# Normed lines of the attention stage: a buffer of their own, written and stored in quarters

## The chip, the cores and the metric

One core of a Trainium2 chip. The metric is device time in microseconds (us), the median of three executions; one further execution was profiled, and all durations below are from that one.

## What is computed

The input x is 8 images of 128 x 128 pixels with 64 channels, float32. Two layers follow each other. The first is criss-cross attention: each pixel attends to its column and to its row.

```python
energy_H = jnp.einsum('bhwd,bkwd->bhwk', Q, K)      # diagonal set to -inf
energy_W = jnp.einsum('bhwd,bhvd->bhwv', Q, K)
att = softmax(concatenate([energy_H, energy_W], axis=-1), axis=-1)
x = gamma[0] * (out_H + out_W) + x                  # sums of V by both parts of att
```

The second layer begins with a normalization over the channels, `(x - mu) * rsqrt(var + EPS)`, and goes on with a two-dimensional Fourier transform, a dense layer with GELU, the inverse transform and a convolutional MLP. The change lies between the two: in the lines of normed x that the first layer leaves for the second.

## The kernel before

Two stages run one after the other, `attention` and `mixer`. Between them lie two arrays in HBM: x2, the result of the attention, and xn, the same with the inverse root of the variance multiplied in, in the order [row, half of the columns, channel, 64 columns].

**Tasks.** The attention goes through 64 tasks: 8 images, for each image four blocks of 32 columns ("H", numbered H0 to H3 here) and then four blocks of 32 rows ("W", W0 to W3). A block of the input is one buffer xb of 128 x 2048. W blocks come from a pool of six such buffers (`a_xw`), four used per image, in rotation. Each task spreads over several turns of a loop (lines 599 to 657), which works on several tasks at once. In turn n:

- PE turns the xb of task n + 1 round (`turn`, L348), computes queries, keys and values for it and its energies (L433); DVE takes their maxima (L438), ACT the exponential (L444).
- PE multiplies attention and values for task n, and ACT copies the sums from PSUM to SBUF (`attend`, L403 and L409): into yh for an H block, into yw for a W block. The pool has two yw buffers, each for a pair of W blocks (W0 with W1, W2 with W3). So the first pair of an image takes the buffer of the first pair of the image before. PSUM has four buffers, and the energies need one that L409 has emptied.
- POOL computes the difference of the maxima for task n (`maximum`, L484), ACT the weights for task n - 1 (`weigh`, L514 to L516), POOL their totals (L522 to L524), and POOL merges task n - 2 (`combine`): for each eighth of the block it scales yh and yw (L541), adds each to xb (L544), and stores xb to x2 (L545).
- ACT and DVE square and sum the xb of task n - 4 (L559 to L562); the squares go to yw, whose sums are used up by then.
- POOL takes the inverse root for task n - 5 (`inverse_root`, L89 to L105) and, where that task is the second of a pair, multiplies both blocks of the pair by it (L574, eight instructions of 128 x 512, four for each block) and stores the pair (L578, 2048 KB). The products are written into the same yw buffer, ordered by channel.

At the begin of each image's W blocks PE also turns yh round in place (`across`, L584 and L585); L497 is the copy just ahead of that, and occurs once per image.

**Order.** On PE, ACT, DVE and POOL the order of instructions is the program's. The fetches of xb (L265 for H, L268 for W) are on SP's queue, in an order that the scheduler chose: four of H, then four of W, in turn. A W fetch waits until the last reader of its buffer is through, so the fetches of W2 and W3 of an image wait for the products of W0 and W1 of the image before, and those of W0 and W1 of the next image for the products of W2 and W3. For the last three tasks, DVE and SP take the place of POOL (`merger`, `store`), so 14 pairs are multiplied and stored by POOL and two by DVE and SP.

Of the kernel before, what the change touches and what calls it, by code (L numbers as in the profile page):

```python
# [22 lines left out]
F32 = mybir.dt.float32  # L23
# [3 lines left out]
ALU = mybir.AluOpType  # L27
# [4 lines left out]
P = 128  # L32
C = 64
D8 = 8
HID = 128
R = 32
# [49 lines left out]
def inverse_root(engine, fused, s, q, t):  # L86

    e = engine
    e.tensor_tensor(t, s, s, ALU.mult)  # L89
    e.tensor_scalar(q, q, 1.0 / C, EPS, ALU.mult, ALU.add)  # L90
    if fused:
        e.scalar_tensor_tensor(out=q, in0=t, scalar=-1.0 / (C * C), in1=q, op0=ALU.mult, op1=ALU.add)
    else:
        e.tensor_scalar(t, t, -1.0 / (C * C), None, ALU.mult)
        e.tensor_tensor(q, q, t, ALU.add)
    e.tensor_scalar(s.bitcast(I32), q.bitcast(I32), -0.5, float(0x5F3759DF), ALU.mult, ALU.add)
    e.tensor_scalar(q, q, -0.5, None, ALU.mult)
    for _ in range(3):
        e.tensor_tensor(t, s, s, ALU.mult)
        e.tensor_tensor(t, t, q, ALU.mult)  # L100
        if fused:
            e.scalar_tensor_tensor(out=s, in0=t, scalar=1.5, in1=s, op0=ALU.add, op1=ALU.mult)
        else:
            e.tensor_scalar(t, t, 1.5, None, ALU.add)
            e.tensor_tensor(s, s, t, ALU.mult)  # L105
# [136 lines left out]
def attention(tc, nc, x, w_q, b_q, w_k, b_k, w_v, b_v, gamma, x2, xn, prm, marks, packed):  # L242
    NB = x.shape[0]
    with ExitStack() as ctx:
# [4 lines left out]

        late = ctx.enter_context(tc.tile_pool(name="a_late", bufs=2))  # L250
        xw = ctx.enter_context(tc.tile_pool(name="a_xw", bufs=6))

        ps = ctx.enter_context(tc.tile_pool(name="a_ps", bufs=4, space=PSUM))

# [71 lines left out]
        for n in range(3):  # L326
            m = const.tile([P, 4, 32], F32, tag="m%d" % n, name="m")
# [119 lines left out]
        state = {}  # L447
# [52 lines left out]
        def merger(n):  # L500

            return nc.vector if n >= len(tasks) - 3 else nc.gpsimd
# [5 lines left out]
        def is_w(n):  # L508
            return 0 <= n < len(tasks) and tasks[n][1] == "W"
# [37 lines left out]
        def norm_step(n, part):  # L547


            m = n - 4  # L550
            if is_w(m):
                s = state[m]
                h = slice(16 * (part // 2), 16 * (part // 2) + 16)
                sq = s.y[:, h, 0:C]
                if part % 2 == 0:
                    if m >= N - 3:
                        nc.vector.tensor_tensor(sq, s.xb[:, h, :], s.xb[:, h, :], ALU.mult)
                    else:
                        nc.scalar.activation(sq, s.xb[:, h, :], AF.Square)  # L559
                    nc.vector.tensor_reduce(s.t[:, 0, h], s.xb[:, h, :], AX.X, ALU.add)  # L560
                else:
                    nc.vector.tensor_reduce(s.t[:, 1, h], sq, AX.X, ALU.add)  # L562
            m = n - 5
            if is_w(m):
                b, way, blk = tasks[m]
                s = state[m]
                r, q, t = (s.t[:, i, :] for i in range(3))
                if part == 3:
                    inverse_root(merger(m), m >= N - 3, r, q, t)
                if part == 3 and blk % 2 == 1:  # L570
                    z = s.yw.rearrange("p r c -> p (r c)")[:, 0 : 2 * R * C].rearrange("p (c r) -> p c r", c=C)
                    for o, lo in ((state[m - 1], 0), (s, R)):
                        for h in range(0, R, 8):
                            merger(m).tensor_tensor(  # L574
                                z[:, :, lo + h : lo + h + 8].rearrange("p c r -> p r c"), o.xb[:, h : h + 8, :],
                                o.t[:, 0, h : h + 8].unsqueeze(2).to_broadcast([P, 8, C]), ALU.mult,
                            )
                    (nc.sync if m >= N - 3 else nc.gpsimd).dma_start(out=xn[b][:, blk // 2, :, :], in_=z)  # L578

        def across(o, c0):  # L580

# [14 lines left out]
        N = len(tasks)  # L596
        E = mybir.EngineType
        with tc.manual_schedule(engines={E.PE, E.Activation, E.DVE, E.Pool}):
            for n in range(-1, N + 6):
# [31 lines left out]
                if new is not None or old is not None:  # L631
                    for k in range(2):
                        energies(0, k, new, old, masked)
                norm_step(n, 0)
                if is_w(n - 1):
                    weigh(n - 1)
                if new is not None:
                    new.values(1)
                norm_step(n, 1)
                if old is not None:  # L640
                    target(n)
# [3 lines left out]
                if new is not None or old is not None:  # L645
                    for k in range(2):
                        energies(1, k, new, old, masked)
                norm_step(n, 2)
                if is_w(n - 1):
                    total(n - 1)  # L650
# [679 lines left out]
@with_exitstack  # L1330
def attention_mixer_kernel(ctx: ExitStack, tc: tile.TileContext, x, w_q, b_q, w_k, b_k, w_v, b_v, gamma, *rest):
    nc = tc.nc
    *prm, tbl, marks, out = rest
    NB = x.shape[0]
    dram = ctx.enter_context(tc.tile_pool(name="dram", bufs=1, space=DRAM))
    x2 = [dram.tile([P, P, C], F32, tag="x2_%d" % b, name="x2_%d" % b) for b in range(NB)]
    xn = [dram.tile([P, 2, C, 64], F32, tag="xn_%d" % b, name="xn_%d" % b) for b in range(NB)]
    packed = dram.tile([P, PACKED + ADDED], F32, tag="packed", name="packed")

    spread = dram.tile([32, C], F32, tag="spread", name="spread")  # L1340
    nc.sync.dma_start(out=spread, in_=prm[-1].unsqueeze(0).to_broadcast([32, C]))
    attention(tc, nc, x, w_q, b_q, w_k, b_k, w_v, b_v, gamma, x2, xn, prm, marks, packed)
    mixer(tc, nc, x2, xn, tbl, packed, spread, out)
# [32 lines left out]
```

## Time and profile before

| what | us |
|---|---|
| median of three runs | 3188.97 (3185.77 to 3190.28) |
| the profiled execution | 3192.64 |
| its span | 3190.9 |
| PE busy | 2919.0 (91%) |
| DVE busy | 2470.8 (77%) |
| ACT busy | 2097.3 (66%) |
| POOL busy | 1640.7 (51%) |
| L574, POOL, 112 multiplies of 128 x 512, mean | 1.1 each |
| L578, POOL, 14 stores of 2048 KB, issue to landing | 9.5 each |

The shares are means over two stages with different limits: attention ends near 1350 us, and the mixer, with DVE busy nearly throughout, takes the rest. A line of a wait reads "who waited <- for whom: us in total, times, the longest". In a timeline a line gives start, duration, engine, line of the program, operation, tiles (written <- read), and in brackets the idle time before it with what ended it. The chain of waits is followed back from the last instruction, at each step to what released it. PEld is PE's loading of weights, POOLq and SPq are the queues of POOL and SP.

### The profile page before, as it was taken

Reading aid. Unit: us, or ns where it says so; the run is one execution under the profiler, and the core shown is the slowest. Engines: PE = TensorE matmul, PEld = TensorE weight load, DVE = VectorE, ACT = ScalarE, POOL = GpSimd, SP = SyncE. Lnnn points to the kernel's source line nnn. Section 1 sums busy time; section 2 is a strip of 40 time slices with the busy share of each in tenths; the row PEclk is TensorE's granted clock in tenths of the full one; section 3 lists DMA queues with packets and bytes.
Section 4 is the critical chain, followed back from the end, with each engine's and each line's share of the span. In section 5 each row is a group of like instructions: output and inputs, shape, how many; then the busy total and the mean of one; then the engine's idle time right before and its main releaser. Section 6 shows DMA issues by size and latency. Waiting matters only on the chain.

```text
span 3190.9 us, 110456 instructions
## 1 busy us (share of the span) xinstructions
PE 2919.0 (91%) x50476; PEld 2138.6 (67%) x50476; DVE 2470.8 (77%) x2281; ACT 2097.3 (66%) x2776; POOL 1640.7 (51%) x1974
## 2 busy tenths in 40 slices
PE   7998989898989896999999999999999999999978
PEld 5777777777767775676566575575675675665644
DVE  4575747474747577819999999999999999999996
ACT  3665656565656664538868867767867777777754
POOL 1095959595959585424625516515525525435421
PEclk8999999999999998999999999999999999999989
DMA  6024242424243323242674664654745745745545
GB/s 175 23 96 121 96 134 95 121 96 124 102 138 106 112 95 115 89 159 54 137 166 87 157 146 83 172 117 93 179 106 111 171 99 113 179 94 101 119 90 100
DMA packets 227070, 372.72 MB, mean 117 GB/s; under 512 B 143401, under 2 KB 176812, under 8 KB 208044
## 3 DMA queue, kind: packets, MB, share of 16 engines
q0 software_dynamic: 37072, 188.39, 26.0%
q1 hardware_dynamic: 188764, 177.19, 19.7%
q8 instruction: 396, 6.49, 0.8%
q14 instruction: 70, 0.57, 0.1%
q10 hardware_dynamic: 768, 0.07, 0.0%
HBM read 170.96 MB, written 102.26 MB: 86 GB/s over the span
## 4 chain that ended last, share of the span: by engine, by line
PE 40%; DVE 28%; POOL 18%; issue 6%; DMA 5%; ACT 3%; SPq 0%; POOLq 0%; ACTq 0%; DVEq 0%
DVE acc L1144 19%; POOL xb L544 7%; PE fcps L838 5%; PE dps L906 3%; PE yp L403 3%; PE yps L893 3%; PE e L433 3%; POOL yh L541 3%; POOL yw L541 3%; PE yps L895 3%; DMA acc<-pr 3%; PE op L1206 2%; PE tpy L584 2%; PE vps L381 2%; DMA xn<-yw 2%
## 5 line engine op out<-in xcount | busy, mean ns | idle before, releaser
L1144 DVE SCALAR_TENSOR_TENSOR acc<-h,pk,acc 128x1024 f32<-128x1024 f32 x840 | 1262.6, 1509 | 51.2 <-ACT acc L1130 29.6
L854 POOL TENSOR_TENSOR gs<-gl 128x512 f32<-128x512 f32 (+2 forms) x272 | 447.8, 1665 | 296.7 <-ACT gl L848 295.7
L838 PE MATMUL fcps<-f,pk 128*128 128x512 f32 (+2 forms) x1088 | 506.7, 596 | 0.2 <-ACT f L828 0.2
L438 DVE TENSOR_REDUCE m<-e 128x8 f32<-128x1024 f32 x256 | 302.8, 1214 | 209.4 <-PE e L433 204.8
L444 ACT ACTIVATE att<-e 128x1024 f32<-128x1024 f32 x256 | 259.8, 1024 | 163.6 <-PE e L433 159.7
L848 ACT ACTIVATE gl<-fcps,pk 128x1024 f32<-128x1024 f32 (+2 forms) x272 | 290.0, 1073 | 95.2 <-PE fcps L838 75.6
L433 PE MATMUL e<-qt,kt 32*128 32x128 f32 x4096 | 301.4, 291 | 40.5 <-ACT yw L409 35.2
L1039 POOL TENSOR_TENSOR xc<-x,st 128x512 f32<-128x512 f32 x128 | 181.9, 1436 | 297.0 <-PE tpn L1073 120.3
L1138 POOL DMA_DIRECT2D acc<-pr x120 | 105.6, 880 | 434.6 <-DVE acc L1144 253.0
L403 PEld LDWEIGHTS yp<-v,att 128*64 128x64 f32 x8192 | 264.6, 140 | 88.7 <-issue 41.0
L838 PEld LDWEIGHTS fcps<-f,pk 128*128 128x128 f32 x1088 | 190.8, 192 | 195.0 <-issue 145.2
L433 PE MATMUL e<-kt,qt 32*128 32x128 f32 x4096 | 305.6, 291 | 7.8 <-issue 4.3
L403 PE MATMUL yp<-v,att 128*64 128x65 f32 x8192 | 294.2, 227 | 19.2 <-issue 17.4
L433 PEld LDWEIGHTS e<-qt,kt 32*128 32x128 f32 x4096 | 261.1, 195 | 46.7 <-ACT yw L409 36.5
L433 PEld LDWEIGHTS e<-kt,qt 32*128 32x128 f32 x4096 | 264.3, 195 | 21.3 <-issue 9.3
L384 DVE TENSOR_TENSOR v<-vps,bv 128x1024 f32<-128x1024 f32 x128 | 156.4, 1222 | 90.5 <-PE vps L381 90.4
L820 PE MATMUL fps<-tb,at 128*64 128x128 f32 x1008 | 201.6, 283 | 23.3 <-DVE ot L1211 23.3
L1134 ACT ACTIVATE pr<-h,pk 128x1024 f32<-128x1024 f32 x176 | 214.3, 1237 | 0.0
L878 PEld LDWEIGHTS gps<-pk,gs 128*64 128x64 f32 x4032 | 135.8, 143 | 108.5 <-POOL gs L854 51.8
L1115 ACT ACTIVATE h<-hp,pk 128x512 f32<-128x512 f32 x254 | 156.4, 670 | 71.2 <-PE hp L1095 71.2
L893 PE MATMUL yps<-tb,gt 128*64 128x128 f32 x1024 | 201.1, 279 | 0.6 <-ACT gt L887 0.6
L821 PE MATMUL fps<-tb,at 128*64 128x128 f32 x1008 | 201.6, 283 | 0.0
(218 smaller groups left out, 7433.5 us busy)
## 6 DMA issues: line engine op xcount, KB each, us to landing
acc<-pr POOLq DMA_DIRECT2D x120, 512.0 KB, 5.5
xb<-in_x_dram SPq DMA_DIRECT2D x32, 1024.0 KB
xn<-xn SPq DMA_DIRECT2D x32, 1024.0 KB
x<-x SPq DMA_DIRECT2D x32, 1024.0 KB
x<-spread POOLq DMA_DIRECT2D x32, 1024.0 KB, 8.4
x<-xb POOLq DMA_DIRECT2D x30, 1024.0 KB, 5.8
out_dram<-ot SPq DMA_DIRECT2D x120, 256.0 KB
xn<-yw POOLq DMA_DIRECT2D x14, 2048.0 KB, 9.5
```

The lines of the kernel that those rows point to most:

```text
L403: nc.tensor.matmul(yq[z, q, j, :], lhsT=att[:, q, j, z], rhs=self.v[:, r, :], start=True, stop=True)
L433: nc.tensor.matmul(e[:, q, j, :], lhsT=left[rows, 4 * a + j, :], rhs=right[rows, 4 * a + j, :], start=not msk, stop=j == 3 or not msk,)
L438: nc.vector.tensor_reduce(new.mneg[:, 2 * k : 2 * k + 2, 4 * a : 4 * a + 4], e1, AX.X, ALU.max, negate=True,)
L444: nc.scalar.activation(att, e2, AF.Exp)
L544: merger(n).tensor_tensor(xv, xv, part, ALU.add)
L820: nc.tensor.matmul(fps[0:64, n, :], lhsT=re, rhs=cos, start=True, stop=False)
L838: nc.tensor.matmul(ps[:, sgn, 0:n], lhsT=w[:, cols], rhs=fv, start=True, stop=not mean)
L848: nc.scalar.activation(gl[:, :, 0:n], ps[:, :, 0:n], AF.Gelu, bias=bfc[:, half : half + 1])
L854: nc.gpsimd.tensor_tensor(gs[:, 0:n], gl[:, 0, 0:n], gl[:, 1, 0:n], ALU.add if half == 0 else ALU.subtract)
L893: nc.tensor.matmul(yps[0:64, c, :], lhsT=gr, rhs=cosn, start=True, stop=False)
L1134: nc.scalar.activation(pr, self.lines(k, t), AF.Identity, bias=zero, scale=wdw[:, t : t + 1])
L1144: nc.vector.scalar_tensor_tensor(out=a, in0=self.lines(k, t), scalar=wdw[:, t : t + 1], in1=a, op0=ALU.mult, op1=ALU.add)
```

## The change

A pool of three buffers of 128 x 16 x 64 (4 KB per partition each) is added. For the pairs that POOL multiplies, sixteen channels of both blocks are multiplied into one such buffer (two instructions, each over 32 rows and 16 channels) and stored with a DMA of their own (512 KB); this is done four times per pair, with the buffers in rotation. yw is no longer written by this step. The pairs of the last tasks stay as they were, on DVE and SP.

```diff
         xw = ctx.enter_context(tc.tile_pool(name="a_xw", bufs=6))
+        lines = ctx.enter_context(tc.tile_pool(name="a_lines", bufs=3))
...
                 if part == 3 and blk % 2 == 1:
+                    if m < N - 3:
+
+                        for c in range(0, C, 16):
+                            z = lines.tile([P, 16, 2 * R], F32, tag="z", name="z")
+                            for o, lo in ((state[m - 1], 0), (s, R)):
+                                nc.gpsimd.tensor_tensor(
+                                    z[:, :, lo : lo + R].rearrange("p c r -> p r c"), o.xb[:, :, c : c + 16],
+                                    o.t[:, 0, :].unsqueeze(2).to_broadcast([P, R, 16]), ALU.mult,
+                                )
+                            nc.gpsimd.dma_start(out=xn[b][:, blk // 2, c : c + 16, :], in_=z)
+                        return
                     z = s.yw.rearrange("p r c -> p (r c)")[:, 0 : 2 * R * C].rearrange("p (c r) -> p c r", c=C)
                     for o, lo in ((state[m - 1], 0), (s, R)):
                         for h in range(0, R, 8):
-                            merger(m).tensor_tensor(
+                            nc.vector.tensor_tensor(
                                 z[:, :, lo + h : lo + h + 8].rearrange("p c r -> p r c"), o.xb[:, h : h + 8, :],
                                 o.t[:, 0, h : h + 8].unsqueeze(2).to_broadcast([P, 8, C]), ALU.mult,
                             )
-                    (nc.sync if m >= N - 3 else nc.gpsimd).dma_start(out=xn[b][:, blk // 2, :, :], in_=z)
+                    nc.sync.dma_start(out=xn[b][:, blk // 2, :, :], in_=z)
```

## The prediction

> **What bounds the kernel now.** I began with the page's forty slices (80 us each). Attention fills the first sixteen: POOL alternates between full and half, and only later does DVE stay at 9.
>
> ```profile
> PE   7998989898989896999999999999999999999978
> DVE  4575747474747577819999999999999999999996
> POOL 1095959595959585424625516515525525435421
> ```
>
> The change is in attention, so everything below is read there, from 0 to 1230 us. Next, the waits, in total, times, longest:
>
> ```profile
> ACT yw L409 <- DMA xn<-yw: 55.0, 6, 10.7
> ...
> PE e L433 <- ACT yw L409: 35.2, 7, 7.6
> PE vps L381 <- issue: 17.6, 10, 3.0
> PE yp L403 <- issue: 17.4, 14, 3.8
> ```
>
> ACT may not copy new sums into yw until the store of normed lines that lie in that buffer has landed. PE then waits for ACT, because ACT frees PSUM. "Issue" on PE is a wait for nothing that the profile shows. The chain of waits, image 1, says that this is the path (start, us, what):
>
> ```profile
> 253.94 7.13 POOL yw L574 x7
> 261.06 0.29 issue
> 261.35 9.69 DMA xn<-yw
> ...
> 271.13 0.60 ACT yw L409
> 271.73 0.04 issue
> 271.78 3.64 PE e L433 x60
> ```
>
> The stretches from one image's L497 to the next (us; then busy us and count of PE, PEld, DVE, ACT, POOL; clock; DMA share; GB/s) show what an image costs without the wait. Image 0 finds both yw buffers new:
>
> ```profile
> 115.90:257.40 141.50, 135.38 (x3662) 112.39 (x3666) 95.26 (x84) 93.22 (x121) 90.99 (x129) 1.00 0.18 63
> 257.40:409.50 152.10, 139.62 (x3666) 115.93 (x3669) 95.05 (x84) 92.97 (x122) 112.50 (x178) 0.97 0.36 114
> ```
>
> Last, the timelines of POOL and SP about the store, for what else hangs on it:
>
> ```profile
> 252.93 8.12 POOL L574 TENSOR_TENSOR yw<-xb,tsm 128x512 f32<-128x512 f32 x8
> 261.35 0.62 POOL L578 DMA_DIRECT2D xn<-yw  x1 [0.30 <-POOL yw L574]
> ...
> 282.99 0.28 POOL L484 TENSOR_TENSOR tsm<-mdt,m 128x32 f32<-128x32 f32 x1
> 257.10 0.69 SPq L268 DMA_DIRECT2D xb<-in_x_dram  x1
> 261.13 0.78 SPq L268 DMA_DIRECT2D xb<-in_x_dram  x1
> ```
>
> SP's two fetches leave just when the first four and the last four multiplies are through. They bring the next image's blocks W2 and W3 into the xb buffers that these multiplies read (six buffers, four used per image).
>
> So attention is a loop of an image's length. I count from c, the first L541 of an image's combine (162.07, 314.74, 469.34, 621.62, 777.68, 931.41, 1083.37, 1234.97): seven periods, mean 1072.9/7 = 153.3 us. POOL starts the first pair's multiplies at c+91.0 without a gap of note, its store lands at c+109, PE turns block W2 (L348; 276.5, 429.3, 583.7, 737.0, 892.6, 1046.5, 1197.7) at c+114.7, and from there it is 38.6 to the next c (36.9 to 40.7). In image 0 that last leg took 162.07 - 128.5 = 33.6: it has no store and no issue wait.
>
> [...] the trace has 9.5 (2 MB, L578) and 5.5 (512 KB, acc<-pr), and those I use. [...] while the 2 MB store moved in 16 KB packets, the W3 fetch in its 1 KB packets crawled. [...] the trace has 8.12/8 = 1.0. [...] PEclk is 0.50 at 269 to 273, and a 32x128 energy matmul takes 0.42 us after the stall, 0.28 before.
>
> **The change, part by part.** *Removed*: ACT's wait on the store, in seven images (L409 lists six on the DMA and one more of 9.6 that it puts down to POOL). The order of instructions on PE, DVE, ACT and SP is the same in both programs; L409 waits for PE alone. yw's other readers are long through: L562 on DVE ran by 217. With no stall PE would follow image 0: L497 to W2's turn took 128.5 - 115.9 = 12.6, L497 is at c+94.2 on average, so PE wants W2 at c+106.8 instead of c+114.7.
>
> *Multiplies*: 8 of 128x512 per pair stay 8, now in runs of 16 elements instead of 64. Small runs show no price in the trace: L484 in runs of 8 takes 259 ns, flat L522 254. I take 1.0. A gain is excluded, since elements, operands and engine are the same; above I allow 1.2.
>
> *Issues*: 4 instead of 1 per pair, each 0.30 wait + 0.62 issue + 0.02 to the next instruction = 0.94. The wait also takes the overlap of neighbours from the multiplies: two alone last 1.0 + 1.1 = 2.1. So a quarter lasts 3.05, and a pair's multiplies end 3 x 3.05 + 2.1 = 11.3 after their start instead of 8.1: 3.2 us more, for each of 14 pairs. After the second pair POOL is idle (283 to 313.6 in image 1), which hides 2 x 3.2 = 6.4 an image; without that cover it would be 45 us in all. Queued behind are L484 for W0 and W1; ACT uses them at 289 and 313, over 20 us later. But the first pair's 3.2 is not hidden, as follows.
>
> *The fetch*: each quarter now reads both blocks, so both xb buffers come free only with the last quarter. That ends at 91.0 + 11.3 = c+102.3; W2's fetch leaves at c+102.4 instead of c+95.0. By the trace's DMA packets such a first fetch took 6.5 to 7.8 from issue to last data, mean 7.0; it now meets the last quarter's store, 512 KB at the 390 KB/us of the 2 MB store: 1.3. So W2 lands at 102.4 + 7.0 + 1.3 = c+110.7, 3.9 later than PE wants it. This is what is late next: PE turns W2 at c+110.8, a gain of 3.9. [...] W3 follows some 5 us later and is wanted 20 us on. The next image's W0 and W1 leave at about c+126 instead of c+116 and c+120, and are wanted a hundred us later; SP's H fetches behind them began at 319.7 anyway.
>
> *The ring of three*: quarter 3 waits for quarter 0's store. Issued at 91.0 + 2.4 = 93.4, landed at +5.5 = 98.9; wanted at 91.0 + 3 x 3.05 = 100.2. Free. Bounds: [...] 9.5 (the whole store's) 2.7 per image.
>
> *The last leg*, 38.6, holds the cold clock's tail and most issue waits: 2.9 us in image 1, 3.8 in image 2, and like ones later, all 6 to 12 us after the second 2 MB store. Stores of 4 KB packets in four parts should crowd PE less, yet fetches of xb alone had such waits too (2.1 to 2.7 at 37 to 67 us). Between 33.6 (all gone) and 38.6 (none) I take 36.5.
>
> Sum: 110.8 + 36.5 = 147.3 against 153.3: 6.0 us x 7 = 42 us. The profiled execution took 3192.6 (span 3190.9), so 3150.6; the median of the runs is 3.7 lower: **3147 us**. After 1230 us nothing moves but the start; the last image's pairs stay on DVE and SP. Beside this, the bounds: multiplies at 1.2 take 1.6 x 7 = 11 us back, the ring up to 19, and the leg alone is worth 2.9 x 7 = 20 more to 2.1 x 7 = 15 less.
>
> **Rivals.** *A, stores in parts free PE altogether*: the leg falls to 33.6. 110.8 + 33.6 = 144.4, 8.9 x 7 = 62: **3127**. For it: every long issue wait follows a z store. Against: those at 37 to 67 us. Below lies PE's own floor, image 0's 141.5: 11.8 x 7 = 82, 3107, for which W2 would have to land 4.4 us after its issue; no fetch did.
>
> *B, the fetch takes the place of the wait*: W2 shares the engines with the stores as W3 did, 12.6 to 13.2 us from issue. 102.4 + 12.9 = c+115.3, with a leg of 36.5 to 38.6: 151.8 to 153.9, **3178 to 3193**, middle 3186. For: W3's times. Against: much of these was waiting behind W2's fetch, and a quarter's store is 512 KB, not 2 MB.
>
> *C, slower*: runs of 16 cost POOL more. At 2.3 us a multiply the first pair ends 8 x 1.3 = 10.4 later, and so does W2's fetch: 121.2 + 36.5 = 157.7, 4.4 x 7 = 31 longer, **3220**. It decides from 1.0 + 6.0/8 = 1.75 us. Against: L484's runs of 8.
>
> That the change doesn't do what it says can be left out: in the changed program L409 no longer waits for a store.
>
> **How the numbers follow.** Forecast 0.50 (3133 to 3163); A 0.20 (3107 to 3133); B 0.21 (3163 to 3193); C 0.09. About 0.2%, 6.4 us, is what a measurement of this kernel can tell. 3112 to 3180 leaves out the bottom of A (0.02), the upper part of B (0.09) and C (0.09). Faster by over 6.4: forecast, A and two thirds of B, 0.84; within: 0.07, from B; slower: 0.09.
>
> **What would show it.** L409 without waits on a DMA; the multiplies at 1.0 us spacing and four issues of about 0.6 per pair; SP's first W fetch of a pair directly after the last multiply; PE's turn of W2 waiting 2 to 4 us for the xb fetch; periods of c near 147. I am wrong if the turn waits 8 us or more, if quarter 3 waits for its buffer, if multiplies take over 1.2, or if PE's issue waits stay whole or vanish.

## The result, and the profile after

| | before | after |
|---|---|---|
| median of six runs each, same chip, us | 3189.62 (3185.77 to 3198.26) | 3137.27 (3130.29 to 3146.01) |
| ratio after / before | | 0.9833, 95% interval 0.9809 to 0.9857 |
| the profiled execution, us | 3192.64 | 3130.29 |
| its span, us | 3190.9 | 3128.2 |

The median fell by 52 us, where 42 were forecast. The profiled execution of after happens to be the shortest of its six; its gain of 62 us is more than the median's, and a section below separates what belongs to the kernel.

In after the lines of attention have numbers that are one or more higher (L348 is L349, L409 is L410); the multiplies are now L577, their stores L581. First POOL's line of the forty slices of after's page:

```profile
POOL 1097979787877875415525425425435435445421
```

POOL's valleys in attention are at 7 instead of 5: it issues four stores for one, and the period got shorter. The waits of after from 0 to 1230 us (total, times, longest):

```profile
ACT yw L410 <- PE yp L404: 43.1, 65, 1.5
...
PE tp L349 <- DMA xb<-in_x_dram: 19.6, 7, 6.9
...
PE yp L404 <- issue: 8.8, 13, 2.1
...
PE e L434 <- issue: 8.2, 9, 2.0
...
PE vps L382 <- issue: 4.4, 5, 2.3
```

What ACT waits for before it copies into yw is PE and, as in before, a small step on DVE (49.2 us, 46.8 before): the 55.0 us on the store are gone, and so are PE's 35.2 us on ACT. In their place stands the fetch of a block; 6.9 of its 19.6 us belong to the start of the kernel, so six images wait 12.7 us. Of the issue waits, those at vps fell from 17.6 to 4.4 and those at yp from 17.4 to 8.8, while the energies' stayed (9.0 before). The chain of waits of after (start, us, what) runs through a fetch where the prediction's chain ran through the store; the multiplies are those of the second image, and the turn of block W2 of the third image waits:

```profile
392.41 2.12 POOL z L577 x2
394.53 0.29 issue
394.82 0.62 POOL xn L581
...
401.51 1.11 POOL z L577
402.69 8.01 DMA xb<-in_x_dram
410.70 0.14 issue
410.83 1.94 PE tp L349 x16
```

The last multiplies of the pair lead to the fetch of W2, and that to PE's turn. The timeline of POOL shows the quarter that the prediction worked with, 3.05 us from issue to issue (394.82, 397.85, 400.90):

```profile
395.46 2.09 POOL L577 TENSOR_TENSOR z<-xb,tsm 128x512 f32<-128x512 f32 x2
397.85 0.60 POOL L581 DMA_DIRECT2D xn<-z  x1 [0.30 <-POOL z L577]
398.46 2.13 POOL L577 TENSOR_TENSOR z<-xb,tsm 128x512 f32<-128x512 f32 x2
400.90 0.59 POOL L581 DMA_DIRECT2D xn<-z  x1 [0.30 <-POOL z L577]
401.51 2.15 POOL L577 TENSOR_TENSOR z<-xb,tsm 128x512 f32<-128x512 f32 x2
```

And the instructions of the tile z, with the landing of its stores:

```profile
L577 POOL TENSOR_TENSOR z<-xb,tsm x112: 1065/1118/1162, 248.4 to 1151.9; 128x512 f32<-128x512 f32 x112
...
DMA to landing us min/median/max: 3.0/3.6/8.4
```

Where the time went, by stretch: start to the first c, the seven periods, the rest. The columns are as in the prediction (us; then busy us and count of PE, PEld, DVE, ACT, POOL; clock; DMA share; GB/s). Before:

```profile
0.00:162.07 162.07, 138.68 (x3347) 113.69 (x3349) 81.96 (x100) 76.18 (x95) 17.43 (x50) 0.94 0.37 98
162.07:1234.97 1072.90, 975.76 (x25612) 809.82 (x25610) 666.63 (x588) 650.65 (x848) 791.88 (x1246) 0.97 0.34 109
```

After:

```profile
0.00:157.53 157.53, 137.31 (x3347) 111.99 (x3349) 81.81 (x100) 76.29 (x95) 17.43 (x49) 0.95 0.38 100
157.53:1170.70 1013.17, 961.56 (x25613) 797.79 (x25611) 665.85 (x588) 654.24 (x848) 822.37 (x1289) 0.99 0.36 115
```

So 59.7 us of the profiled difference come from the seven periods, 4.5 from the start and -1.6 from the rest (1955.9 before, 1957.5 after). In the periods PE does the same 25,612 matmuls, yet it is busy 14.2 us less and its clock is 0.99 instead of 0.97. That is a part of the gain that the sum in the prediction had no term for.

### The profile page after: what moved, and what is told of

Read it like the earlier page. It is cut to its first block, busy times and chain, and to the rows that moved or that the text cites. A ratio compares the mean times of both kernels' runs of the same rounds, so it can differ in the third digit from the quotient of the medians.

```text
span 3128.2 us, 110509 instructions
## 1 busy us (share of the span) xinstructions
PE 2905.1 (93%) x50476; PEld 2127.9 (68%) x50476; DVE 2471.3 (79%) x2281; ACT 2101.5 (67%) x2776; POOL 1668.1 (53%) x2016
## 4 chain that ended last, share of the span: by engine, by line
PE 41%; DVE 23%; POOL 22%; DMA 5%; issue 5%; ACT 3%; SPq 0%; POOLq 0%; ACTq 0%; DVEq 0%
DVE acc L1156 16%; POOL xb L545 9%; PE fcps L850 6%; POOL yh L542 4%; POOL yw L542 4%; PE dps L918 4%; PE yps L905 3%; PE yps L907 3%; PE op L1218 3%; PE yp L404 2%; DMA acc<-pr 2%; PE gps L890 2%; PE e L434 2%; PE hp L1107 2%; PE tpy L596 2%
## 5 line engine op out<-in xcount | busy, mean ns | idle before, releaser
L404 PEld LDWEIGHTS yp<-v,att 128*64 128x64 f32 x8192 | 261.0, 139 | 80.3 <-PE pq L363 38.5
L434 PE MATMUL e<-kt,qt 32*128 32x128 f32 x4096 | 290.7, 283 | 7.3 <-issue 3.4
L434 PE MATMUL e<-qt,kt 32*128 32x128 f32 x4096 | 289.4, 281 | 5.4 <-issue 4.9
L434 PEld LDWEIGHTS e<-kt,qt 32*128 32x128 f32 x4096 | 251.8, 187 | 20.2 <-issue 7.9
L434 PEld LDWEIGHTS e<-qt,kt 32*128 32x128 f32 x4096 | 249.1, 186 | 10.3 <-issue 5.4
L832 PE MATMUL fps<-tb,at 128*64 128x128 f32 x1008 | 201.8, 283 | 23.4 <-DVE ot L1223 23.4
L890 PEld LDWEIGHTS gps<-pk,gs 128*64 128x64 f32 x4032 | 136.6, 143 | 109.6 <-POOL gs L866 53.4
L905 PE MATMUL yps<-tb,gt 128*64 128x128 f32 x1024 | 202.7, 280 | 0.6 <-ACT gt L899 0.6
L906 PE MATMUL yps<-tb,gt 128*64 128x128 f32 x1024 | 202.8, 280 | 0.0
```

The costliest lines, as they stand in the source:

```text
L404: nc.tensor.matmul(yq[z, q, j, :], lhsT=att[:, q, j, z], rhs=self.v[:, r, :], start=True, stop=True)
L434: nc.tensor.matmul(e[:, q, j, :], lhsT=left[rows, 4 * a + j, :], rhs=right[rows, 4 * a + j, :], start=not msk, stop=j == 3 or not msk,)
L905: nc.tensor.matmul(yps[0:64, c, :], lhsT=gr, rhs=cosn, start=True, stop=False)
```

## The experiments

**How they are read.** The gain lies in seven periods, so each kernel's profiled execution is cut there, from its first c to its eighth. PE's time in that stretch is what it waits plus its own time; of the waits the table names those on ACT for yw, on the fetch of a block (xb), and issue waits; 15 to 19 us of small ones are in the total. "Half clock" is how long the granted clock stood at 0.5. The rest is from the eighth c to the end. All in us, the first two rows being the kernel before (twice), the next two the change (twice). Each row is one execution: the change itself took 1013.2 us in one and 1029.0 in the other, so a smaller difference between single rows shows nothing by itself.

| run | seven periods | PE waits | yw | xb | issue | PE's own | half clock | the rest | median of runs |
|---|---|---|---|---|---|---|---|---|---|
| before | 1072.9 | 94.1 | 35.2 | 0 | 42.2 | 978.8 | 71.7 | 1955.9 | 3189.6 |
| e8_before_again | 1068.5 | 92.9 | 32.8 | 0 | 42.7 | 975.6 | 71.7 | 1954.2 | 3184.5 (one) |
| after | 1013.2 | 47.4 | 0 | 12.7 | 18.0 | 965.8 | 27.3 | 1957.5 | 3137.3 |
| e7_change_again | 1029.0 | 61.0 | 0 | 12.2 | 32.7 | 968.0 | 34.1 | 1948.2 | 3137.5 |
| e6_four_att_padded | 1026.7 | 57.6 | 0 | 16.1 | 26.1 | 969.1 | 34.1 | 1958.4 | 3135.1 |
| e1_third_yw | 1010.7 | 50.7 | 0 | 0 | 33.5 | 960.0 | 17.1 | 2004.1 | 3187.6 |
| e2_quarters_in_yw | 1063.7 | 91.8 | 50.6 | 0 | 25.6 | 971.9 | 78.5 | 1959.1 | 3183.2 |
| e4_one_line | 1076.4 | 95.3 | 0 | 54.9 | 23.3 | 981.1 | 88.7 | 1955.7 | 3196.3 |
| e0_four_att | 1021.2 | 54.7 | 0 | 10.3 | 28.2 | 966.5 | 23.9 | 2015.7 | 3188.2 |
| e5_first_block_first | 1015.8 | 51.1 | 0 | 0 | 34.7 | 964.7 | 30.7 | 1956.1 | 3138.2 |
| e3_seven_xb | 1007.4 | 45.3 | 0 | 0 | 26.8 | 962.1 | 17.1 | 1993.6 | 3162.2 |
| e9_seven_xb_turned | 1020.6 | 51.7 | 0 | 0 | 35.9 | 968.9 | 37.5 | 1990.9 | 3172.7 |
| e10_small_stores | 1010.8 | 46.7 | 0 | 16.9 | 14.1 | 964.1 | 23.9 | 1959.7 | 3130.1 |
| e11_before_small_stores | 1016.6 | 49.8 | 5.1 | 0 | 28.4 | 966.8 | 27.3 | 1961.4 | 3138.0 |

The theory to be tested: the change gains by taking away the wait on yw, gives part of it back to the late fetch of W2, and gains on the last leg because stores in parts crowd PE less. The rival: the buffer has nothing to do with it, and stores in parts do it all; or the other way round.

**The buffer alone** (e1_third_yw). Before, with a third yw buffer and the 2 MB store left whole. Room is made with an attention buffer.

```diff
-    flat = lambda: pool.tile([P, 2 * R, C + 1], F32, tag="yw", name="pk").rearrange("p r c -> p (r c)")
+    flat = lambda: pool.tile([P, 2 * R, C + 1], F32, tag="yw", name="pk", bufs=3).rearrange("p r c -> p (r c)")
...
-                att = p4.tile([P, 2, 4, P], F32, tag="att", name="att", bufs=5)
+                att = p4.tile([P, 2, 4, P], F32, tag="att", name="att", bufs=4)
...
-                    o.yw = late.tile([P, 2 * R, C + 1], F32, tag="yw", name="yw")
+                    o.yw = late.tile([P, 2 * R, C + 1], F32, tag="yw", name="yw", bufs=3)
```

> The kernel before with a third yw buffer and nothing else of the change: the normed lines still go into yw and leave in one store of 2 MB (one buffer of the exponentials is given up for the room). My theory: both parts of the change pay, the buffer in the turn of W2 and the small stores in the last leg. Here ACT does not wait, the fetch of W2 leaves at c+95 as before and is early, PE turns W2 at c+107 to 108, and the last leg stays at 38.5: period 145 to 147, about 3135 to 3145 us. Rival 1, the buffer does all and the leg was only shortened because PE no longer stalls: leg 35, period 142, about 3115. Rival 2, the parts of the store did it all: 3180 or more.

In the whole it gave 3187.57 us, 0.9983 of before (0.996 to 1.0007). In the seven periods it took 1010.7, no worse than the change (its profiled execution was 10 us below the median of its runs): PE waits on yw no more, the mean turn of W2 was at c+108.5 and the leg 35.9. So the wait on the buffer alone explains the gain there. The leg was expected to stay at 38.5, since the 2 MB stores were whole; it fell with the wait, and its issue waits from 22 to 12.2 us. That the buffer does it all in attention, and the parts nothing that can be told from the scatter, is thus not excluded. The gain was lost later, after attention (2004.1 against 1955.9), as the waits of e1_third_yw from 1172 to 1400 us show:

```profile
ACT f L828 <- DMA xn<-yw: 48.4, 1, 48.4
...
PE fcps L838 <- ACT f L828: 46.4, 1, 46.4
```

**The parts alone** (e2_quarters_in_yw). Before, with quarters of sixteen channels, but written into yw.

```diff
+                    if m < N - 3:
+                        for c in range(0, C, 16):
+                            for o, lo in ((state[m - 1], 0), (s, R)):
+                                nc.gpsimd.tensor_tensor(
+                                    z[:, c : c + 16, lo : lo + R].rearrange("p c r -> p r c"), o.xb[:, :, c : c + 16],
+                                    o.t[:, 0, :].unsqueeze(2).to_broadcast([P, R, 16]), ALU.mult,
+                                )
+                            nc.gpsimd.dma_start(out=xn[b][:, blk // 2, c : c + 16, :], in_=z[:, c : c + 16, :])
+                        return
```

> The kernel before with the multiplies and stores in quarters, but still written into yw. My theory: the last quarter lands at c+106 (multiplies end at c+102.2, 0.3, then 3.6 as measured for such a store) instead of c+109, so ACT still waits, some 5 us instead of 8; PE turns W2 at c+112, the leg falls to 35 because the stores are small: period 147, about 3145 us. Rival 1, the buffer alone pays: the leg stays at 38.5, period 150.5 or more, 3170 or more. Rival 2, the parts did it all: 3137, as with the change.

3183.18 us, 0.9966 (0.9949 to 0.9983). The issue waits fell from 42 to 25.6 us and the leg from 38.3 to 35.4, but the wait on yw grew from 34 to 50.6, and the period was 152.0 where 147 was expected:

```profile
PE e L433 <- ACT yw L409: 50.6, 7, 9.1
```

The last quarter is issued at c+102.5 and lands at c+111, 8 us or more later and not 3.6; the fetches of W2 and W3 leave beside it, at c+101.3 and c+102.4. The rival "parts do it all" falls: without a buffer of their own they give 7 us of the seven periods' 48.

**One line buffer instead of three** (e4_one_line): each quarter waits for the landing of the one before.

```diff
-        lines = ctx.enter_context(tc.tile_pool(name="a_lines", bufs=3))
+        lines = ctx.enter_context(tc.tile_pool(name="a_lines", bufs=1))
...
-                att = p4.tile([P, 2, 4, P], F32, tag="att", name="att", bufs=5)
+                att = p4.tile([P, 2, 4, P], F32, tag="att", name="att", bufs=4)
```

> The changed kernel with one line buffer instead of three, so that each quarter waits for the store before it. A quarter then lasts 2.1 + 0.3 + 3.6 = 6.0 instead of 3.05, the first pair's multiplies end at c+111.2 instead of c+102. My theory: the fetch of W2 after the last multiply sets the turn of W2, which comes 9 us later, at c+118 to 119; with a leg of 35 the period is 153 to 154, about 3200 us, no better than before though yw is free. Rival, the fetch is not on the path and ACT's wait was all: about 3137, as with three.

3196.31 us, 1.0005 (0.999 to 1.0019): the whole gain is gone. ACT never waits on yw, yet the last multiply ends some 9 us later, the fetch of W2 leaves at c+110.4 and PE turns W2 at c+118.0. The waits of e4_one_line from 0 to 1230 us:

```profile
PE tp L349 <- DMA xb<-in_x_dram: 61.7, 8, 10.8
```

This shows rival B's and C's path to be real: what delays the multiplies delays the fetch and PE with it. The time came out as expected.

**The control** (e0_four_att): the change with four attention buffers instead of five, as in the two runs above.

```diff
-                att = p4.tile([P, 2, 4, P], F32, tag="att", name="att", bufs=5)
+                att = p4.tile([P, 2, 4, P], F32, tag="att", name="att", bufs=4)
```

> The changed kernel with four instead of five buffers of the exponentials, a control: other experiments need that room. I expect no difference, 3130 to 3146 us and periods near 144.7. If it costs something, the periods of the experiments with four are to be read against this one.

The control did not come out as expected: 3188.21 us, 0.9991 (0.9978 to 1.0004). The periods are those of the change (1021.2), but the rest takes 2015.7. The waits of e0_four_att from 1182 to 1400 us:

```profile
ACT f L840 <- DMA xn<-yw: 49.0, 1, 49.0
```

It is the mixer's first copy into f, which now waits for attention's last store. A reason for this can be read in the addresses that the program gives its buffers, which stand in no trace: a buffer of 4 KB less moves all later attention buffers by 4 KB, and the mixer's f and gl then reach into memory that attention uses to its end (gl into yh), where before and after they lie over H blocks. **The control with the addresses kept** (e6_four_att_padded) puts 4 KB of idle memory into the same pool:

```diff
+        spare = p4.tile([P, 16, 2 * R], F32, tag="spare", name="spare", bufs=1)
+        nc.gpsimd.memset(spare[:, 0, 0:1], 0.0)
```

> The change with four attention buffers instead of five, and 4 KB of idle memory put in their pool, so that every later buffer keeps its address. If the loss of the first control at the handover to the mixer came from the shift of addresses, this one is the change again: periods of 144.5 to 146 us, about 1957 us from the last c to the end, 3137 us in all (3125 to 3150). If the fifth attention buffer itself was worth the 50 us, it is about 3188 us again, with the mixer's first activation waiting some 49 us.

3135.07 us, 0.9832 (0.9807 to 0.9856), the rest 1958.4: it is the change again. So the fifth buffer is worth nothing, and the 50 us of e0 come from the addresses; those of e1, with the same wait at the same place, most likely too. A third yw buffer would have been as good in attention; what it costs is 16.25 KB and its place.

**How much one execution tells** (e7_change_again, e8_before_again): both kernels unaltered, once more.

> The changed kernel once more, unaltered, beside the others on this chip: periods of 144 to 146 us, 3137 us (3130 to 3146). It shows how much the last leg and TensorE's waits without a cause differ from one profiled execution to the next: if the leg is 35.2 us again within 0.7, the legs of single runs can be compared; if it differs by 1.5 us or more, the 3.4 us that the leg gave in the result are partly the run's luck.

> The kernel before once more, for a second profiled execution. The changed kernel's three profiled executions (two of the change, one with padded memory) had 18, 33 and 26 us of issue waits on TensorE in the seven periods, the kernel before 42 us in its only one, and its clock was at half for 72 us against 27 to 34 us. If both belong to the kernel and not to that one execution, this one has 38 us or more of issue waits, 60 us or more at half clock, a leg of 38 to 39 and seven periods of 1066 to 1080 us. If the first execution was unlucky, the leg falls to 36 or less and the periods to 1055 us.

The change gave 3137.54 us, 0.9835 (0.9811 to 0.9859). Its leg was 34.9 against 35.2, but its seven periods took 15.8 us more than in the first profile, of which 14.7 are issue waits (32.7 against 18.0). The kernel before repeated itself: a leg of 38.0, issue waits of 42.7 and 71.7 us at half clock. So the leg belongs to the kernels, and the first profile of the change was a lucky one, 7 us below the median.

**Where issue waits come from.** The records of DMA packets hold queues of kind "instruction", and one of them, q8, has blocks of 16 KB: 200 of them in seven periods in before and after alike, which is 64 bytes for each of PE's 51,200 matmuls and weight loads there. From these counts I take them for PE's instructions; no trace shows what they hold. Leaving out waits for a fetched block, all 9 idle stretches of PE over 0.8 us in after, all 15 in e7, all 13 in e6, 13 in e5 and 7 in e10 ended 1.0 to 1.75 us after such a block had landed (200 x 0.75 / 1013: a random moment falls there once in 7 times). In before all 21 did that were not waits on ACT. Ahead of these waits a block had come 8 us after the last one, in the median, against 4.3 us over all blocks. That PE had run out of instructions is my reading of these times; no run shows it apart.

Over the seven periods of all fourteen traces there are 192 such issue waits, and each ended 1.19 to 1.67 us after a block. In the 4 us ahead of that block, other transfers kept the DMA engines busy at 57% or more (79% in the median); ahead of the other 2,614 blocks it was 0% in the median and 23% in the mean. So these waits came where other data moved.

The longest gaps ahead of such waits in before and e8, 10.4 to 13.6 us, end at c+123 to c+128, while the second 2 MB store of an image moved (issued at c+120.3, 9.5 us), and two fetches of blocks from c+116 on. One of the waits that follow in the leg, in the timeline of PE of before:

```profile
447.21 2.53 PE L403 MATMUL yp<-v,att 128*64 128x65 f32 x41 [3.76 <-issue]
```

and the windows about it, where the last three numbers are the clock, the DMA share and GB/s:

```profile
441.00:445.00 4.00, 2.20 (x94) 1.80 (x88) 2.75 (x3) 1.80 (x5) 0.72 (x3) 1.00 1.01 296
445.00:449.00 4.00, 1.79 (x33) 1.79 (x34) 0.00 (x0) 0.59 (x1) 0.00 (x0) 0.60 0.41 86
449.00:453.00 4.00, 4.00 (x53) 3.55 (x55) 0.00 (x0) 1.68 (x2) 0.00 (x0) 0.55 0.00 0
```

PE idles 3.76 us from 443.45 on, and then works at about half clock until 453 (the granted clock stood at 0.5 from 445.8 to 452.6): this wait was paid for twice.

**The stores' bytes** (e10_small_stores, e11_before_small_stores). The change, and the kernel before, with a sixteenth of each store; the mixer loads the sums instead of the normed lines, which both kernels leave out. The question is what the issue waits go with, the stores or the fetches of blocks.

```diff
-                            nc.gpsimd.dma_start(out=xn[b][:, blk // 2, c : c + 16, :], in_=z)
+                            nc.gpsimd.dma_start(out=xn[b][:, blk // 2, c : c + 1, :], in_=z[:, 0:1, :])
...
-                nc.sync.dma_start(out=self.xn[:, :, c, :], in_=xn[self.b][:, :, c, :])
+                nc.sync.dma_start(out=self.xn[:, :, c, :], in_=x2[self.b].rearrange("p (n q) c -> p n q c", n=2)[:, :, c, :])
```

```diff
-                    (nc.sync if m >= N - 3 else nc.gpsimd).dma_start(out=xn[b][:, blk // 2, :, :], in_=z)
+                    (nc.sync if m >= N - 3 else nc.gpsimd).dma_start(out=xn[b][:, blk // 2, 0:4, :], in_=z[:, 0:4, :])
```

> The change with a sixteenth of each store's bytes: each quarter stores one of its sixteen channels, and the mixer loads the same amount from the array of the sums, so the normed lines are left out of the result. Instructions, waits and the order of all queues stay. [...] (issue waits end 1.2 to 1.5 us after a 16 KB block lands on the instruction queue). If the stores do, the issue waits in the seven periods fall from 18 to 33 us to below 10, and the period to 141 to 142.5 us (3115 to 3122). If the fetches of blocks do, the issue waits stay at 15 us or more, and only the fetch of W2 gets quicker: period 143 to 144 us (3125 to 3135).

> The kernel before with a sixteenth of each pair's store (four of 64 channels; the mixer loads the sums in their place, so the normed lines are left out of the result). The buffer, its wait and the single store stay, but the store lands in some 3 us. If the wait on the buffer and the crowding by the 2 MB store are all that the change removes, this comes to or below the change's period, 141 to 144 us, with the turn of W2 at c+105 to 107.5, since here its fetch leaves at c+95: 3110 to 3130 us. If the single buffer holds ACT up even so ([...] the multiplies end at c+99), the turn stays above c+109 and the period above 146 us.

e10: 3130.11 us, 0.9802 (0.9778 to 0.9826); periods of 144.4. By its figures this is the second of the two theories expected (14.1 us of issue waits, where 15 or more were expected, and a time within 3125 to 3135), but hardly for its reason: the data of W2 came 6.7 us after the issue, 7.3 in after. The fetch left at c+101.4 and PE turned W2 at c+109.3, as with full stores (c+109.6 in after), and PE waited 16.9 us for it. All seven issue waits over 0.8 us that are left lie at c+27 to c+65, where no pair is stored, though other transfers run; in e7 and e6 five of 15 and 13 lie after c+100 and hold 10 to 12 us. The median lies 7 us below the change's, which would fit these late issue waits, but the two intervals overlap and after has only 0.9 us of such waits: what full quarters cost is not shown. The waits at c+27 to c+65 are not these stores' doing.

e11: 3137.99 us, 0.9829 (0.9802 to 0.9856), periods of 145.2, leg 35.4. With its bytes cut, the old buffer and its single store are as good as the change. The turn of W2 came at c+109.8, later than expected though its fetch left at c+95: PE lost 20 us to issue waits before the turn. In the leg 7.9 us of them were left, of 22 with the 2 MB store. The change thus removes what the move of 2 MB out of a buffer in use brings with it: PE's wait for that buffer, and most of the issue waits of the leg. How many of these are due to the bytes alone cannot be told from e11, since the wait on yw fell with them; 5.1 us of it are left, with stores that land in 4.3 us.

**The late fetch** (e5_first_block_first, e3_seven_xb, e9_seven_xb_turned). Three ways to let W2's fetch go without waiting for the last multiply, all with four attention buffers as in e6. e5 multiplies the whole first block before the second, in four line buffers (the fourth in the spare 4 KB):

```diff
-                        for c in range(0, C, 16):
-                            z = lines.tile([P, 16, 2 * R], F32, tag="z", name="z")
-                            for o, lo in ((state[m - 1], 0), (s, R)):
+                        parts = [lines.tile([P, 16, 2 * R], F32, tag="z", name="z") for _ in range(3)]
+                        parts.append(p4.tile([P, 16, 2 * R], F32, tag="spare", name="z", bufs=1))
+                        for o, lo in ((state[m - 1], 0), (s, R)):
+                            for n, z in enumerate(parts):
+                                c = 16 * n
...
-                            nc.gpsimd.dma_start(out=xn[b][:, blk // 2, c : c + 16, :], in_=z)
+                                if lo:
+                                    nc.gpsimd.dma_start(out=xn[b][:, blk // 2, c : c + 16, :], in_=z)
```

e3 takes seven block buffers and two line buffers (the second in the spare 4 KB); e9 also uses up five of the seven once at the start:

```diff
-        xw = ctx.enter_context(tc.tile_pool(name="a_xw", bufs=6))
-        lines = ctx.enter_context(tc.tile_pool(name="a_lines", bufs=3))
+        xw = ctx.enter_context(tc.tile_pool(name="a_xw", bufs=7))
+        lines = ctx.enter_context(tc.tile_pool(name="a_lines", bufs=1))
...
-                            z = lines.tile([P, 16, 2 * R], F32, tag="z", name="z")
+                            pool, tag = ((lines, "z"), (p4, "spare"))[c // 16 % 2]
+                            z = pool.tile([P, 16, 2 * R], F32, tag=tag, name="z", bufs=1)
```

```diff
+        for _ in range(5):
+            turn = xw.tile([P, R, C], F32, tag="xw", name="turn")
+            nc.gpsimd.memset(turn[:, 0, 0:1], 0.0)
```

> The four multiplies of the first block of the pair go first, into four line buffers, and then each quarter has its second multiply and its store. So the first block is free four multiplies after the start, at c+95, and the fetch of W2 leaves there as in the kernel before. If TensorE really waits for that fetch in the changed kernel (1.8 us a period), the turn of W2 comes at c+107 to 108 instead of c+109.6, the wait for the block is gone, and with a last leg of 35.2 the period is 142 to 143 us: 15 us in all, about 3122 us (3112 to 3132). If the block's wait stands for something else that is late too, or if the stores and the fetches now collide on the last leg, the period stays at 144.7 and the time at 3137 us.

> The change with seven block buffers instead of six, paid for with one of the three line buffers and one attention buffer (addresses of later stages kept). The fetch of W2 has then a buffer that no multiply reads, and can leave before c+95. If the block is what the turn of W2 waits for, the same as for the other order: turn at c+107 to 108, period 142 to 143, about 3122 us (3112 to 3132). With two line buffers the third multiply waits for the first store's landing, 3.6 us after its issue, at about c+97, some 0.6 us after it would start: the multiplies end less than 2 us later, which nobody waits for here. If the order of the multiplies matters rather than the fetch, it stays at 3137 us.

> Seven block buffers as in the run before of that kind, which took 1007 us for its seven periods but lost 36 us at the handover, where the mixer's first hermite combination waited for the last block's multiplies, whose buffer had come to lie under its own. Here five buffers are taken in turn once at the start, so that the last image's blocks use other buffers than the one under the mixer's. If that was the loss, the handover costs 1957 us again from the last c, and the whole is 3122 to 3130 us, 8 to 15 us less than the change (3137): the late fetch of W2 is then shown to cost the change about that. If the loss stays, 3162 us again.

e5: 3138.17 us, 0.9834 (0.9812 to 0.9856), the change's own time, 16 us above what was expected. Its fetch left at c+95.1, and the wait for the block is gone from the waits of e5_first_block_first (0 to 1230 us; the one left is the start's):

```profile
PE yp L404 <- issue: 14.3, 13, 3.2
PE vps L382 <- issue: 11.5, 6, 3.5
...
PE e L434 <- issue: 9.3, 12, 2.0
PE tp L349 <- DMA xb<-in_x_dram: 6.9, 1, 6.9
```

In its place stand issue waits of PE, 34.7 us in the seven periods, with the turn of W2 at c+109.6 all the same. Five of its 13 long ones lie at c+101 to c+105, where after, e7 and e6 have none; e7 and e6 have three at c+107 to c+108. They follow the fetches of blocks, which start at c+95 in e5 and at c+101 in e7 and e6. e3 had the best seven periods of all (1007.4), e9, the same but for the buffers' turn, 1020.6; neither waits for a block, and their issue waits are 26.8 and 35.9. Over the four kernels without a wait for the block (e1, e3, e5, e9) issue waits average 32.7 us; in after, e7 and e6 issue waits and xb waits together average 39.3. The late fetch is thus worth some 7 us of its 13.7 by these means, which is within the scatter, and in e5's median nothing. No run shows why the issue waits are longer there (32.7 against 25.6 us).

e3 and e9 lose 35 us after attention in another way. The waits of e9_seven_xb_turned from 1150 to 1420 us:

```profile
POOL gs L870 <- DVE yw L590: 53.5, 1, 53.5
```

By the program's addresses the mixer's gs lies where the third line buffer lay, and now a block buffer is there. That its last user were the last image's multiplies was my reason for e9, and it was wrong: the addresses of the last four blocks moved away, the wait stayed at 53.5. Which of attention's readers it needs is open. No complete version among these beats the change.

## Why the prediction was right, and where not

In the means of three profiles of the change (after, e7, e6) against two of before the seven periods went from 1070.7 to 1023.0, by 47.7 us: yw -34.0, issue waits -16.9, xb +13.7, PE's own time -9.6, small ones -0.9. The periods average 146.1 where 147.3 was forecast: the turn of W2 came 3.9 us earlier, as forecast, and the leg is 2.9 us shorter, where 2.1 was forecast.

- *The wait removed* was right: 34 us of PE's time, none left.
- *The multiplies and issues* were right: 1065 to 1162 ns for a multiply, 3.05 us for a quarter, two multiplies beside a store in 2.1. Runs of 16 cost next to nothing, 1.118 us a multiply in the median against 1.106 for the runs of 64 in before, so rival C had no ground.
- *The fetch* was right in kind, with its terms mis-sized. "Both xb buffers come free only with the last quarter" holds for W1's block; W0's last reader is the multiply before the last, so W2's fetch left at c+101.3 and not at c+102.4. Of the 1.3 us for meeting the last store little exists: the data of W2 came 7.3 us after the issue in after, 7.0 in before and 6.7 in e10 with small stores. The turn of W2 came at c+109.6 in after, and at c+110.8 in the mean of three profiles, which is the figure forecast, but partly by luck: PE had lost 16 to 26 us to issue waits ahead of the seven turns. So PE wanted W2 later than c+106.8, and waited 2.0 us a period for it instead of 3.9. Rival B's 12.9 us for the fetch were not seen.
- *The ring of three* was free, as said: a pair's first store, for which quarter 3 waits, landed in 3.1 us in the median and 4.8 at most, not in 5.5 (the profile tells it for 7 of 14). The fourth store, beside the block fetches, took up to 8.4, so that the median over all is 3.6 in after and 5.0 in e7. e4_one_line shows what one buffer costs: everything.
- *The last leg* was mis-sized: 35.3 in the mean of three, not 36.5. This term is 8 of the 10 us between forecast and result. The leg holds 23.1 and 21.8 us of issue waits in before and e8, 2.3 to 6.8 in the change. The prediction took a mean between none gone and all gone; about four fifths went. It put them down to the second 2 MB store, and the runs bear that out in part: with quarters and the wait on yw kept 9.0 are left (e2, leg 35.4), but with the store whole and the wait gone 12.2 (e1, leg 35.9). So the stall ahead of the leg has a share in them for which the prediction had no term; how it acts on them is open.
- *The clock* had no term of its own. The granted clock stood at 0.5 for 3.4, 6.8 or 10.2 us at a time, 71.7 us in all; now for 27 to 34 us, and PE's own time shrank by 9.6 us with it. PE did not idle through the 3.41 us ahead of every fall. Here is the fall ahead of a turn of W2 in after, where PE waited 1.64 us for the block (the windows show the clock behind the engines' busy times):

```profile
841.69:845.10 3.41, 1.79 (x24) 1.41 (x18) 1.69 (x2) 2.52 (x3) 2.59 (x11) 1.00 1.08 279
845.10:848.51 3.41, 3.30 (x16) 3.33 (x17) 0.00 (x0) 1.01 (x1) 2.71 (x12) 0.50 1.09 257
```

The clock fell like this at the waits for the block in five of seven periods of after, at 1.6 to 3.3 us of waiting each. A us of waiting removed was worth 1.25 us (47.7 for 38.2). The prediction had put the tail of the slow clock into the leg; in before it lies at c+105 to c+115, mostly ahead of the turn of W2, and at c+129 to c+138 in the leg.

- Rival A, 62 us, was nearer to the first profile than the forecast was; against the median's 52 the two are equally far off. The mechanism was between them: with the quarters PE is free of most issue waits of the leg, not of all.

## What to carry to other kernels

When a stage's output buffer is also its staging area for a store, look for the next writer of that buffer on the critical engine: in attention three buffers of 4 KB did what a third of 16.25 KB did. Then ask what the new code reads and when it is through, because the next fetch into the buffers that it reads can become the path, as it did here (c+101.3), and price a removed wait above its length where the granted clock falls at it, as it did here to 0.5 at five waits of 1.6 to 3.3 us. Before taking a gain or a loss of a resized buffer as its own, see whether it moved the addresses of a later stage: 4 KB less cost 50 us.

## What the runs showed of the hardware

- TensorE's long issue waits came while DMA moved other data. Blocks of 16 KB on the queue of kind "instruction" landed every 4.3 us in the median, but after 8 us in the median ahead of a standstill, at most 15.1 (in e11, at c+124, with small stores and two block fetches under way); PE then stood still until 1.19 to 1.67 us after a block had landed (192 waits over 0.8 us in fourteen traces), and other transfers kept the DMA engines busy at 57% or more in the 4 us before that block. With 25,600 matmuls in seven periods, issue waits took 14 to 43 us of a loop of 1007 to 1076.
- In the records of before and after the clock granted to TensorE was 1.0 or 0.5, and from one change to the next passed 3.41 us or a multiple of it. In the seven periods of the fourteen traces it fell after 113 windows of that length, in which PE had been busy 0 to 64% (39% in the median), and stayed full after 3,942, in which PE had been busy 42% at least, and 83% or more in 19 of 20.
- A 512 KB store landed about 3.1 us after its issue in the median where it was a pair's first, and 7.4 to 8.4 us after it where two 1 MB fetches started beside it (six stores of after); the one fourth store of a pair in after that had no fetch beside it and whose landing shows took 3.7.
- At the handover of two stages, a tile of the later stage waited 48.4 to 53.5 us for the earlier one in four kernels whose buffers lie elsewhere by some KB (e0, e1, e3, e9), and did not in e6, which is e0 with the addresses kept. This is a matter of the program's buffers more than of the chip.
